# Layer 2's exponentials added by VectorE alone, and a regrouping of copies and gate steps around it, in a four-layer convolution and attention kernel

## Chip, core and metric

The kernel runs on one core of one Trainium2 chip. The metric is the device time of one execution in microseconds, as the median of several executions.

## What is computed

The input x is (4, 256, 48, 48) in float32; gn is a group normalization over groups of 8 channels. Four layers are applied, each as x = x + layer(gn(x)).

```python
# layer 0: attention over 8 heads of 64, queries and keys normalized, 2304 positions
q, k, v = split(w_qkv @ x); out = w_out @ softmax(10 * l2norm(q).T @ l2norm(k)) @ v
# layer 1: gate from a max pool, a blur of stride 3 and four depthwise sums (11x3, 3x11, two skewed)
s = x_h1 + x_w1 + x_h2 + x_w2;  out = x * upsample(sigmoid(batchnorm(s)))
# layer 2: one-head attention over 2304 positions, 64 channels, batch statistics over all samples
f = theta_x @ phi_x * 64 ** -0.5;  y = softmax(f) @ g_x;  out = batchnorm(W_w @ y + W_b)
# layer 3: channel gate, 3x3 depthwise convolution, instance normalization, leaky relu
a = sigmoid(leaky(mean(x) @ w1.T) @ w2.T);  y = conv3x3(x * a) + b;  out = leaky(instancenorm(y))
```

## The kernel before

All instructions are issued by hand in an order that the program fixes; no scheduler moves them. Every engine runs its own queue in that order and waits on semaphores. PE is TensorE, DVE is VectorE, ACT is ScalarE, POOL is GpSimd and SP issues most DMAs.

**Attention (layers 0 and 2).** A unit is 384 query columns of one sample (and, in layer 0, of a pair of heads). It is worked in 9 groups of 2 key blocks of 128; one group is one slot of the loop in `attend`. In a slot, `scores` issues 16 matmul records per group into the PSUM tiles `sc`, ACT takes the exponential into `pt` (a pool of 8 buffers, 128x768 each), `add_up` adds the exponentials of the group before to `acc`, and `weigh` multiplies them with the values into `av`. Layer 0 has 16 phases (4 samples by 4 head pairs) of 6 units; layer 2 has 4 phases (samples) of 3 units.

`add_up` has two ways: groups in `u["paired"]` are first summed on POOL into a `half` tile (line 355), and DVE then adds the half to `acc` (lines 364 and 370); the others are added by DVE one exponential at a time. In layer 0 the pairs are formed for the first sample alone; in layer 2 for all groups of the first three samples and four groups of nine of the last.

**Side work.** `fills` and `due` are tables from slot to jobs. Jobs in `fills` carry a rank: those below 1 run before `add_up`, the others after it, in order of rank. All side products on PE share two PSUM tiles (`pj_tile`), so a product can start only when the tile used two products earlier has been read. In layer 2 the side work is: the next sample's projections (`project2`: `both` for theta and phi, `g` for the values), the statistics of W times y (`w_stats`: 8 matmuls at line 1256 and two `bn_stats` at line 1264), and the whole of layer 1 for the last sample, as generators: `maxima`, the depthwise sums on PE (`strips_pe`, line 1061, from buffers named y, t and w in `ORDER3`), `gated` and its statistics. `follow` then projects the last sample for layer 2. In the last slot of a phase the generators are run to their end. A unit ends with `take` (av to `raw` on ACT), `fold` and `divide` (lines 417 to 423, on POOL, on DVE in the last sample) and a total over `acc` (`total`, or `total_here` at line 429 in the last sample).

**Layer 3.** Tiles are 8 (4 samples by 2 channel halves) of 6 convolution steps each, `products` at line 1884. A step reads shifted copies `sh` of the padded input `pad`: 12 copies for the upper and 12 for the lower half of the rows, 8 of them as DMAs from SP and 4 on engines, placed by `spread_first`, `spread_out` and `keep_here` with the table `HERE`. `grow` (line 1713, DVE) makes the padded input from PE's product at line 1651. Events are sorted by step and by a rank (CONV early, PLACE and LAST late). A chain of small steps per sample (`Chain`, times in `GATE_AT`) makes the channel gate; `scale` (ACT, line 1973), `leak` and `gain` (DVE, lines 1979 and 1984) and `store` finish a tile.

Of the kernel before, what the change touches and what calls it, by code (L numbers as in the profile page):

```python
# [78 lines left out]
def usual_path(  # L79
# [269 lines left out]
    def add_up(u, g):  # L349
# [10 lines left out]
        if g == NG - 1:  # L360
            ready, u["terms"] = ready + u["terms"], []
        if "acc" not in u and len(ready) > 1:
            u["acc"] = apool.tile([P, 2, SL], F32, tag="acc", name="acc")
            nc.vector.tensor_add(u["acc"], ready[0], ready[1])  # L364
            ready = ready[2:]
# [59 lines left out]
    def total_here(u):  # L425

        ps = pj_tile()
        for h, c in enumerate(HALVES):
            nc.tensor.matmul(ps[c, :SL], lhsT=ones, rhs=u["acc"][:, h, :], start=True, stop=True)
        u["rinv"] = rpool.tile([P, SL], F32, tag="rinv", name="rinv")  # L430
        if u.get("final"):
            fold(u, nc.vector)
            row = xsp.tile([P, NK, SL + 1], F32, tag="xs", name="lrow")[:, 0, :SL]
            nc.scalar.copy(row, ps[:, :SL])
        nc.vector.reciprocal(u["rinv"], ps[:, :SL])
        u["l"] = row if u.get("final") else ps

# [24 lines left out]
    def last(u, t):  # L462

        take(u)
        if u.get("soon"):
            todo = [
                (fills, 1, lambda: total_here(u)), (due, 2, lambda: divide(u, nc.vector)),
            ]
            if u.get("final"):
                noted.append(lambda: note(u))  # L470
            else:
                todo.insert(1, (due, 2, lambda: fold(u, nc.vector)))
                todo.append((due, 2, lambda: note(u)))
# [13 lines left out]
    def attend(phases):  # L487
# [59 lines left out]
        pu, pg = prev  # L547
        add_up(pu, pg)
        for j in range(pg * G, (pg + 1) * G):
            weigh(pu, j)  # L550
# [389 lines left out]
    def strips(b, k, norm, res):  # L940
# [52 lines left out]
        (0, 1, "y"), (0, 2, "y"), (0, 3, "y"), (0, 0, "t"), (1, 1, "w"), (1, 0, "t"), (1, 2, "w"),  # L993
        (1, 3, "t"),
    ]
# [126 lines left out]

    def gated(b, k, norm, res):

# [4 lines left out]
        )  # L1129
        yield 1  # L1130
        nc.scalar.activation(gate, acc, AF.Exp, bias=nb1[:, k : k + 1], scale=-1.0)
# [11 lines left out]
        for i in range(4):  # L1143
            if i < 3:
                nc.vector.tensor_mul(xg[:, :, i], xg[:, :, i], up)
            if i > 0:
                nc.vector.tensor_add(xg[:, :, i - 1], xg[:, :, i - 1], up2)
            yield 1


    def project2(b, norm, s2):
# [43 lines left out]
        def both(s):  # L1195
# [16 lines left out]
            )  # L1212
            nc.sync.dma_start(s2["k"][theta, cols], s2["k"][phi, cols])

        def g(s):
# [13 lines left out]
            )  # L1229
            if b == 0 and s + 2 < NSL:  # L1230
                fetch(s + 2)

        return start, [
            [(1, lambda s=s: both(s)), (2 if b else 2.7, lambda s=s: g(s))] for s in range(NSL)
        ]

# [56 lines left out]
    def l2_unit(b, c, s2):  # L1293
        return {
            "pt": {}, "qc": slice(c * SL, (c + 1) * SL), "of": s2, "after": [],
            "paired": PAIRED if b == B - 1 else range(NG), "scale": D ** -0.5,
            "soon": b == B - 1, "final": b == B - 1 and c == L2C - 1,
            "o": lambda: y_of(b)[:, c * SL : (c + 1) * SL],
        }
# [71 lines left out]
    def l1_last(b, ahead):  # L1371
# [29 lines left out]
        def gates():  # L1401
            for k in range(NK):
                yield from until(res[k], "summed")
                yield from gated(b, k, norm, res[k])
                yield from stats(k)
# [21 lines left out]
    def follow(start, slices, norm):  # L1427

        while "nb" not in norm:
            yield 1  # L1430
        yield 2
        start()
# [73 lines left out]
    for b in range(B):  # L1506
        work, others = {}, []

        def stats(b, c):
            return [lambda k=k: w_stats(b, k, c) for k in range(NK)]  # L1510

# [41 lines left out]
    for s in range(NCH):  # L1553
        projs[0]["values"](s)
    projs[1]["norms"]()
    attend(phases)
# [188 lines left out]

    def place(i, h, j, q, how):
        to = shifted[(2 * i + h) % 3][32 * q : 32 * q + 32, j, :CL]
        c0 = h * HB * W2 + SHIFT[j, q]
        fr = pads[i % NPAD][32 * j : 32 * j + 32, c0 : c0 + CL]
        if how == "sp":  # L1750
# [20 lines left out]
    def spread_first(h):  # L1771
# [4 lines left out]
        else:  # L1776
            how = dict.fromkeys(AWAY, "sp")
            how |= {(0, 0): "dve", (1, 1): "pool", (2, 2): "dve", (3, 3): "pool"}
        for (j, q), e in how.items():
            place(0, h, j, q, e)  # L1780

# [241 lines left out]
    def judge():  # L2023
# [20 lines left out]

        return [(0, MID, lows), (2, SMALL, count), (3, MOMENTS, read), (5, MID, compare)]

    GATE_AT = {
        0: (3, 5, 6, 9, 10, 11, 11, 12), B - 1: (-2, -1, 0, 3, 4, 5, 7, 8),
    }
# [19 lines left out]
    for c in range(L2C):  # L2069
        grow(1, c, ahead[c])  # L2070
        square(1, c)
    noted[0]()
    border(1)
# [13 lines left out]
    def put_before(t, i):  # L2087
# [13 lines left out]
        (-6, 0, (0, 1), "dve"), (-5, 0, (2, 3), "dve"),  # L2101
        (-3, 1, (0, 1), "act"), (-2, 1, (2,), "act"), (-2, 1, (3,), "dve"),
    ]

    def put_tile(i, t, cv, final):
# [33 lines left out]
    for i, cv in enumerate(convs):  # L2139
# [4 lines left out]
        if i:  # L2144
            for h in range(2):
                at(max(0, t - 6 + 3 * h), PLACE, lambda i=i, h=h: spread_out(i, h))
            for dt, h, js, how in HERE:
                at(t + dt, PLACE, lambda i=i, h=h, js=js, how=how: keep_here(i, h, js, how))
# [886 lines left out]
```

## Time and profile before

| | us |
|---|---|
| median of 3 executions (lowest, highest) | 3455.24 (3453.64, 3456.24) |
| the profiled execution: its time | 3453.34 |
| its span, first to last instruction | 3451.5 |
| mean granted TensorE clock | 0.997 |

The profile is of one execution. A group row gives the line, engine and operation, output and input, their shapes and the count; then total busy time in us and the mean of one in ns; then the engine's idle time just before, with what ended it. A waits row gives the total in us, the number of waits and the longest. A window row gives the stretch and its length, then the busy time of PE, PE's weight loads, DVE, ACT and POOL with counts, the granted clock, the DMA share and GB/s.

### The profile page before, as it was taken

Reading aid. Unit: us, or ns where it says so; the run is one execution under the profiler, and the core shown is the slowest. Engines: PE = TensorE matmul, PEld = TensorE weight load, DVE = VectorE, ACT = ScalarE, POOL = GpSimd, SP = SyncE. Lnnn points to the kernel's source line nnn. Section 1 sums busy time; section 2 is a strip of 40 time slices with the busy share of each in tenths; the row PEclk is TensorE's granted clock in tenths of the full one; section 3 lists DMA queues with packets and bytes.
Section 4 is the critical chain, followed back from the end, with each engine's and each line's share of the span. In section 5 each row is a group of like instructions: output and inputs, shape, how many; then the busy total and the mean of one; then the engine's idle time right before and its main releaser. Section 6 shows DMA issues by size and latency. Waiting matters only on the chain. (4 is left out here: it accounts for less than half of the span.)

```text
span 3451.5 us, 89291 instructions
## 1 busy us (share of the span) xinstructions
PE 3384.6 (98%) x37966; PEld 1698.6 (49%) x37966; DVE 2539.3 (74%) x3298; ACT 2297.4 (67%) x3690; POOL 828.0 (24%) x734
## 2 busy tenths in 40 slices
PE   8999999999999999999999999999999999899988
PEld 5555555555545444544454445554444444444533
DVE  3455545568788788687888787878887878857777
ACT  5565655555886687557866885569768855454577
POOL 2433333320111111011110010101010114777434
PEclk9999999999999999999999999999999999999999
DMA  2211111111111111131111011111111110230067
GB/s 91 50 23 27 22 27 22 27 22 27 20 32 22 27 22 22 31 73 22 27 21 24 15 31 18 31 18 27 22 27 18 29 21 8 58 66 11 9 154 229
DMA packets 111593, 127.25 MB, mean 37 GB/s; under 512 B 42912, under 2 KB 101648, under 8 KB 110416
## 3 DMA queue, kind: packets, MB, share of 16 engines
q1 hardware_dynamic: 109936, 119.53, 17.3%
q8 instruction: 300, 4.92, 0.6%
q10 hardware_dynamic: 1248, 1.91, 0.2%
q14 instruction: 109, 0.89, 0.1%
HBM read 56.99 MB, written 11.80 MB: 20 GB/s over the span
## 5 line engine op out<-in xcount | busy, mean ns | idle before, releaser
L330 ACT ACTIVATE pt<-sc 128x768 f32<-128x768 f32 x1944 | 1473.6, 810 | 757.9 <-PE sc L324 751.4
L370 DVE TENSOR_TENSOR acc<-acc,pt 128x768 f32<-128x768 f32 x1368 | 1367.3, 1000 | 145.3 <-ACT pt L330 51.7
L344 PE MATMUL av<-pt,v 64*64 64x384 f32 x13824 | 1274.8, 484 | 0.0
L324 PE MATMUL sc<-q,k 64*64 64x384 f32 x13824 | 1270.0, 482 | 0.5 <-ACT pt L330 0.5
L324 PEld LDWEIGHTS sc<-q,k 64*64 64x64 f32 x13824 | 525.3, 133 | 589.6 <-issue 556.5
L344 PEld LDWEIGHTS av<-pt,v 64*64 64x64 f32 x13824 | 518.2, 133 | 568.4 <-issue 521.5
L421 POOL TENSOR_TENSOR o<-o,rinv 128x384 f32<-128x384 f32 x95 | 123.7, 1302 | 1710.1 <-DMA rinv<-rinv 1700.0
L355 POOL TENSOR_TENSOR half<-pt 128x768 f32<-128x768 f32 x189 | 370.7, 1966 | 488.0 <-ACT pt L330 405.3
L739 DVE SCALAR_TENSOR_TENSOR x<-pj,bo,x 128x384 f32<-128x384 f32 x192 | 118.5, 617 | 344.2 <-ACT row L388 186.9
L951 ACT ACTIVATE prod<-pd,wt 128x256 f32<-128x256 f32 x486 | 340.5, 761 | 0.2
L370 DVE TENSOR_TENSOR acc<-acc,half 128x768 f32<-128x768 f32 x171 | 187.5, 1097 | 167.8 <-POOL half L355 166.7
L625 PE MATMUL pj<-xs,w 128*128 128x384 f32 (+1 forms) x720 | 275.4, 505 | 0.0
L625 PEld LDWEIGHTS pj<-xs,w 128*128 128x128 f32 x720 | 124.1, 189 | 127.9 <-ACT v L664 34.3
L324 PE MATMUL sc<-qv,kd 64*64 64x384 f32 x1728 | 167.3, 492 | 2.9 <-ACT pt L330 2.8
L974 DVE TENSOR_REDUCE prod<-prod 128x256 f32<-128x1280 f32 x114 | 168.7, 1480 | 0.9 <-ACT prod L951 0.9
L344 PE MATMUL av<-pt,qv 64*64 64x384 f32 x1728 | 167.1, 490 | 0.0
L723 PE MATMUL pj<-o,wo 128*128 128x384 f32 (+1 forms) x384 | 161.4, 502 | 2.3 <-DVE x L739 2.0
L659 PEld LDWEIGHTS pj<-w,xs 128*128 128x128 f32 x1080 | 134.4, 191 | 24.2 <-issue 1.2
L364 DVE TENSOR_TENSOR acc<-pt 128x768 f32<-128x768 f32 x99 | 116.4, 1176 | 39.5 <-ACT pt L330 39.4
L659 PE MATMUL pj<-w,xs 128*128 128x128 f32 x1080 | 134.9, 275 | 0.0
L417 POOL TENSOR_TENSOR o<-raw 128x384 f32<-128x384 f32 x95 | 121.6, 1280 | 43.6 <-ACT raw L413 42.5
L413 ACT COPY raw<-av 128x768 f32<-128x768 f32 x108 | 86.4, 800 | 48.2 <-PE av L344 47.7
(304 smaller groups left out, 2227.6 us busy)
## 6 DMA issues: line engine op xcount, KB each, us to landing
xs<-in_x_dram SPq DMA_DIRECT2D x90, 384.0 KB
sh<-pad SPq DMA_DIRECT2D x126, 162.2 KB
rinv<-rinv SPq DMA_DIRECT2D x208, 94.5 KB
out_dram<-x SPq DMA_DIRECT2D x23, 384.0 KB
w<-in_wqkv_dram SPq DMA_DIRECT2D x32, 192.0 KB
x<-in_x_dram SPq DMA_DIRECT2D x4, 1152.0 KB
x<-in_x_dram SPq DMA_DIRECT2D x9, 384.0 KB
rinv<-ls SPq DMA_DIRECT2D x208, 1.5 KB
```

The costliest lines, as they stand in the source:

```text
L324: nc.tensor.matmul(ps[c * D : (c + 1) * D, h, :SL], lhsT=u["of"]["k"][r, j0 : j0 + D], rhs=u["of"]["q"][r, u["qc"]], start=True, stop=True,)
L330: nc.scalar.activation(pt, ps[:, :, :SL], AF.Exp, scale=u["scale"])
L344: nc.tensor.matmul(u["av"][h * D : (h + 1) * D, half, :SL], lhsT=value(u, j, h)[r], rhs=pt[r, h, :], start=j == 0, stop=j == JB - 1,)
L355: nc.gpsimd.tensor_add(half, pts[0], pts[1])
L370: nc.vector.tensor_add(u["acc"], u["acc"], term)
L417: eng.tensor_add(u["sum"], u["raw"][:, 0, :], u["raw"][:, 1, :])
L421: eng.tensor_mul(o, o, u["rinv"])
L625: nc.tensor.matmul(ps[:, :n], lhsT=at["w"][:, k, t, :], rhs=xs[s][:, k, :n], start=k == 0, stop=k == NK - 1,)
L659: nc.tensor.matmul(ps[:, i * P : (i + 1) * P], lhsT=xs[s][:, k, i * P : (i + 1) * P], rhs=at["w"][:, k, 2, :], start=k == 0, stop=k == NK - 1,
L723: nc.tensor.matmul(ps[:, :n], lhsT=wo[:, p, k * P : (k + 1) * P], rhs=o["o"][:, :n], start=True, stop=True,)
L951: nc.scalar.activation(bufs[n % 3][:, :, min(n, 1) + i].rearrange("p (r c) -> p r c", c=AS), pd[:, PAD + dr : PAD + dr + AS, PAD + dc : PA ...
L974: nc.vector.tensor_reduce(to, bufs[n % 3][:, :, : min(n, 1) + len(taps)], AX.X, ALU.add)
```

## The change

In layer 2 no group is paired any more: DVE adds every exponential. The last unit's last group is not added by DVE at all: `total_here` sums it on PE and is issued before the last `weigh`, and the row copy for the final check is issued on ACT after `take`. `w_stats` gets rank 0.5. In the projections of the first sample `g` goes before `both`. `gated` yields less often in the last sample, `follow` starts a slot earlier, and one stack of the depthwise sums uses the y buffer. In layer 3 the first tile's upper copies are made in two parts (500 and 798 columns), two of its lower copies are made by DVE later, each tile's lower copy j = 1 goes from ACT to DVE a step later, the last tile's lower copies are all on DVE, the last gate chain's sum over groups comes a step later, and a comparison of the final check moves to a later rank. `of_k.clear()` gives one small product its own PSUM tile.

```diff
@@ -361,2 +361,5 @@
             ready, u["terms"] = ready + u["terms"], []
+            if u.get("final"):
+                u["loose"] = ready
+                return
         if "acc" not in u and len(ready) > 1:
@@ -427,11 +430,12 @@
         ps = pj_tile()
-        for h, c in enumerate(HALVES):
-            nc.tensor.matmul(ps[c, :SL], lhsT=ones, rhs=u["acc"][:, h, :], start=True, stop=True)
+        terms = [u["acc"], *u.get("loose", ())]
+        for i, term in enumerate(terms):
+            for h, c in enumerate(HALVES):
+                nc.tensor.matmul(
+                    ps[c, :SL], lhsT=ones, rhs=term[:, h, :], start=i == 0,
+                    stop=i == len(terms) - 1,
+                )
         u["rinv"] = rpool.tile([P, SL], F32, tag="rinv", name="rinv")
-        if u.get("final"):
-            fold(u, nc.vector)
-            row = xsp.tile([P, NK, SL + 1], F32, tag="xs", name="lrow")[:, 0, :SL]
-            nc.scalar.copy(row, ps[:, :SL])
         nc.vector.reciprocal(u["rinv"], ps[:, :SL])
-        u["l"] = row if u.get("final") else ps
+        u["l"] = ps
 
@@ -464,5 +468,9 @@
         take(u)
+        if u.get("final"):
+            row = xsp.tile([P, NK, SL + 1], F32, tag="xs", name="lrow")[:, 0, :SL]
+            nc.scalar.copy(row, u["l"][:, :SL])
+            u["l"] = row
         if u.get("soon"):
             todo = [
-                (fills, 1, lambda: total_here(u)), (due, 2, lambda: divide(u, nc.vector)),
+                (due, 2, lambda: fold(u, nc.vector)), (due, 2, lambda: divide(u, nc.vector)),
             ]
@@ -471,3 +479,3 @@
             else:
-                todo.insert(1, (due, 2, lambda: fold(u, nc.vector)))
+                todo.insert(0, (fills, 1, lambda: total_here(u)))
                 todo.append((due, 2, lambda: note(u)))
@@ -548,2 +556,3 @@
         add_up(pu, pg)
+        total_here(pu)
         for j in range(pg * G, (pg + 1) * G):
@@ -993,3 +1002,3 @@
         (0, 1, "y"), (0, 2, "y"), (0, 3, "y"), (0, 0, "t"), (1, 1, "w"), (1, 0, "t"), (1, 2, "w"),
-        (1, 3, "t"),
+        (1, 3, "y"),
     ]
@@ -1122,3 +1131,3 @@
 
-    def gated(b, k, norm, res):
+    def gated(b, k, norm, res, brief=False):
 
@@ -1129,3 +1138,4 @@
         )
-        yield 1
+        if not brief:
+            yield 1
         nc.scalar.activation(gate, acc, AF.Exp, bias=nb1[:, k : k + 1], scale=-1.0)
@@ -1147,3 +1157,4 @@
                 nc.vector.tensor_add(xg[:, :, i - 1], xg[:, :, i - 1], up2)
-            yield 1
+            if not brief or i % 2:
+                yield 1
 
@@ -1213,2 +1224,4 @@
             nc.sync.dma_start(s2["k"][theta, cols], s2["k"][phi, cols])
+            if b == 0 and s + 2 < NSL:
+                fetch(s + 2)
 
@@ -1229,7 +1242,6 @@
             )
-            if b == 0 and s + 2 < NSL:
-                fetch(s + 2)
 
         return start, [
-            [(1, lambda s=s: both(s)), (2 if b else 2.7, lambda s=s: g(s))] for s in range(NSL)
+            [(1, lambda s=s: both(s)), (2, lambda s=s: g(s))] if b else
+            [(1, lambda s=s: g(s)), (2.7, lambda s=s: both(s))] for s in range(NSL)
         ]
@@ -1295,3 +1307,3 @@
             "pt": {}, "qc": slice(c * SL, (c + 1) * SL), "of": s2, "after": [],
-            "paired": PAIRED if b == B - 1 else range(NG), "scale": D ** -0.5,
+            "paired": (), "scale": D ** -0.5,
             "soon": b == B - 1, "final": b == B - 1 and c == L2C - 1,
@@ -1403,3 +1415,3 @@
                 yield from until(res[k], "summed")
-                yield from gated(b, k, norm, res[k])
+                yield from gated(b, k, norm, res[k], brief=True)
                 yield from stats(k)
@@ -1430,3 +1442,3 @@
             yield 1
-        yield 2
+        yield 1
         start()
@@ -1509,3 +1521,3 @@
         def stats(b, c):
-            return [lambda k=k: w_stats(b, k, c) for k in range(NK)]
+            return [(0.5, lambda k=k: w_stats(b, k, c)) for k in range(NK)]
 
@@ -1554,2 +1566,3 @@
         projs[0]["values"](s)
+    of_k.clear()
     projs[1]["norms"]()
@@ -1745,6 +1758,6 @@
 
-    def place(i, h, j, q, how):
-        to = shifted[(2 * i + h) % 3][32 * q : 32 * q + 32, j, :CL]
+    def place(i, h, j, q, how, part=slice(0, CL)):
+        to = shifted[(2 * i + h) % 3][32 * q : 32 * q + 32, j, part]
         c0 = h * HB * W2 + SHIFT[j, q]
-        fr = pads[i % NPAD][32 * j : 32 * j + 32, c0 : c0 + CL]
+        fr = pads[i % NPAD][32 * j : 32 * j + 32, c0 + part.start : c0 + part.stop]
         if how == "sp":
@@ -1777,5 +1790,7 @@
             how = dict.fromkeys(AWAY, "sp")
-            how |= {(0, 0): "dve", (1, 1): "pool", (2, 2): "dve", (3, 3): "pool"}
-        for (j, q), e in how.items():
-            place(0, h, j, q, e)
+            how |= {(1, 1): "pool", (3, 3): "pool"}
+        top = (RS + 2) * W2
+        for part in (slice(0, CL),) if h else (slice(0, top), slice(top, CL)):
+            for (j, q), e in how.items():
+                place(0, h, j, q, e, part)
 
@@ -2044,6 +2059,6 @@
 
-        return [(0, MID, lows), (2, SMALL, count), (3, MOMENTS, read), (5, MID, compare)]
+        return [(0, MID, lows), (2, SMALL, count), (3, MOMENTS, read), (9, LAST, compare)]
 
     GATE_AT = {
-        0: (3, 5, 6, 9, 10, 11, 11, 12), B - 1: (-2, -1, 0, 3, 4, 5, 7, 8),
+        0: (3, 5, 6, 9, 10, 11, 11, 12), B - 1: (-2, 0, 1, 4, 4, 5, 7, 8),
     }
@@ -2071,2 +2086,3 @@
         square(1, c)
+    keep_here(0, 1, (0, 2), "dve")
     noted[0]()
@@ -2101,4 +2117,5 @@
         (-6, 0, (0, 1), "dve"), (-5, 0, (2, 3), "dve"),
-        (-3, 1, (0, 1), "act"), (-2, 1, (2,), "act"), (-2, 1, (3,), "dve"),
+        (-3, 1, (0,), "act"), (-2, 1, (2,), "act"), (-2, 1, (3,), "dve"), (-1, 1, (1,), "dve"),
     ]
+    HERE_LAST = [*HERE[:2], (-3, 1, (0, 1), "dve"), (-2, 1, (2, 3), "dve")]
 
@@ -2146,3 +2163,3 @@
                 at(max(0, t - 6 + 3 * h), PLACE, lambda i=i, h=h: spread_out(i, h))
-            for dt, h, js, how in HERE:
+            for dt, h, js, how in HERE_LAST if i == len(convs) - 1 else HERE:
                 at(t + dt, PLACE, lambda i=i, h=h, js=js, how=how: keep_here(i, h, js, how))
```

## The prediction

> **What bounds the kernel now.** First the page's busy times: TensorE (PE) is busy for 98% of the span, so a change gains only where PE idles or runs at a reduced clock.
>
> ```profile
> PE 3384.6 (98%) x37966; PEld 1698.6 (49%) x37966; DVE 2539.3 (74%) x3298; ACT 2297.4 (67%) x3690; POOL 828.0 (24%) x734
> ```
>
> Then the windows view says where. I cut at the first scores of layer 2's four samples (2870.6, 2977.9, 3092.5, 3202.0), the last scores (3282.0), the first full convolution (3305.5) and the last (3429.1). The first columns are length and PE busy; then PEld, DVE, ACT, POOL, clock, DMA.
>
> ```profile
> 0.00:2704.00 2704.00, 2693.83 (x29826) 1357.57 (x29830) 1975.15 (x2572) 1852.82 (x3009) 473.67 (x411) 1.00 0.15 29
> 2704.00:2870.57 166.57, 161.70 (x1959) 77.83 (x1955) 135.06 (x173) 109.16 (x164) 15.08 (x11) 1.00 0.14 22
> 2870.57:2977.90 107.33, 98.62 (x1164) 48.90 (x1160) 99.59 (x110) 53.84 (x81) 73.06 (x38) 0.98 0.14 25
> 2977.90:3092.50 114.60, 107.67 (x1384) 54.62 (x1380) 69.88 (x77) 56.59 (x89) 80.45 (x45) 1.00 0.31 65
> 3092.50:3202.00 109.50, 100.39 (x1196) 53.58 (x1192) 72.53 (x90) 54.34 (x83) 74.73 (x40) 0.95 0.13 21
> 3202.00:3282.00 80.00, 77.88 (x946) 42.74 (x942) 63.59 (x74) 42.23 (x57) 42.35 (x40) 1.00 0.04 5
> 3282.00:3305.50 23.50, 16.34 (x147) 9.46 (x140) 20.12 (x46) 14.83 (x14) 7.54 (x8) 1.00 0.20 49
> 3305.50:3429.10 123.60, 118.11 (x1337) 47.49 (x1337) 89.39 (x127) 106.21 (x188) 59.61 (x143) 1.00 0.88 235
> ```
>
> Length less PE busy: layer 2 idles 8.7, 6.9, 9.1 and 2.1 = 26.8 us, against 10.2 in the first 2704. PE's waits in layer 2:
>
> ```profile
> PE pj L1256 <- DVE bst L1264: 7.2, 4, 3.5
> PE pj L1061 <- DVE bst L1264: 4.0, 2, 2.3
> PE sc L324 <- ACT pt L330: 2.8, 1, 2.8
> PE pj L233 <- DVE bst L1264: 2.5, 1, 2.5
> ```
>
> Behind nearly all stands VectorE (DVE): a projection's PSUM tile is freed by bn_stats late in DVE's queue. Why DVE is late although 74% busy, the groups show: the add that takes 0.96-0.99 us elsewhere (second line: layer 0, POOL nearly idle) takes 1.28 beside POOL's pair sums, and DVE also sat 46 us waiting for them.
>
> ```profile
> L370 DVE TENSOR_TENSOR acc<-acc,half 128x768 f32<-128x768 f32 x74 | 94.8, 1282 | 47.4 <-POOL half L355 46.4
> ...
> L370 DVE TENSOR_TENSOR acc<-acc,pt 128x768 f32<-128x768 f32 x380 | 375.6, 988 | 42.1 <-ACT pt L330 17.5 <-DVE acc L370 0.5
> ...
> L355 POOL TENSOR_TENSOR half<-pt 128x768 f32<-128x768 f32 x93 | 194.6, 2101 | 106.8 <-ACT pt L330 85.4 <-DVE acc L370 9.0 <-DMA stack<-pd 5.3
> ```
>
> The longest wait in the timeline, a 0.95 us add stretched to 2.55 with bn_stats and PE behind it:
>
> ```profile
> 3133.89 4.87 POOL L355 TENSOR_TENSOR half<-pt 128x768 f32<-128x768 f32 x2 [0.96 <-DVE acc L364]
> ...
> 3137.03 2.55 DVE L370 TENSOR_TENSOR acc<-acc,half 128x768 f32<-128x768 f32 x1
> 3139.50 1.02 DVE L1264 BATCH_NORM_STATS2 bst<-pj 128x6 f32<-128x384 f32 x2
> 3139.72 1.80 POOL L355 TENSOR_TENSOR half<-pt 128x768 f32<-128x768 f32 x1 [0.96 <-DVE acc L370]
> 3140.11 2.01 PE L1256 MATMUL pj<-y,Ww 64*64 64x384 f32 x8 [3.51 <-DVE bst L1264]
> ```
>
> **The Trainium skill.** "SBUF — State Buffer", section "Who interferes with whom": a DVE instruction with two SBUF inputs and a GpSimd instruction that reads SBUF exclude each other for a whole instruction. The trace agrees: 2.55 against 0.95. "TensorE: Matmul & The Clock Gate", section "What's actually happening": an idle window of about 3.4 us halves PE's clock. The trace halves it already after waits of 2.8, 3.5 and 2.5 us: the clock is 0.73, 0.66 and 0.79 over the 6.4, 10 and 8 us around them, a further loss near 1.7, 3.4 and 1.7 us.
>
> **The change, part by part** (minus is faster).
>
> *Exponentials on DVE alone.* POOL loses 93 pair sums (194.6 us). DVE's adds per unit go from 8 (three units in each of samples 0-2) and 13 (last sample) to 17, the final unit 15: 111 to 202, +91. Free of POOL each costs 0.96 us. The other DVE work of the four windows, taken row by row at its duration where POOL rests (L893 1.38 us, here 2.66; L917 0.58, here 2.09; L260 0.16, here 1.78), sums to 44, 27, 30 and 22 us. POOL work that stays (73.1 - 59.4 = 13.7 us in the first window, about 24, 18 and 18 after; half sums at 2.05) still blocks: in the first window DVE exceeds its free sum by 99.6 - (23 x 0.96 + 44) = 33 us over 73 us of POOL, 0.45 each. DVE after:
> - first: 51 x 0.96 + 44 + 6 = 99 us, PE 98.6: a tie. DVE, not PE, may set the pace. Of the 8.7 idle and 1.7 clock I take -4 (bounds -8 to +6).
> - second: 49 + 27 + 11 = 87 of PE 107.7. Waits of 1.5, 2.3 and 1.9 go: -5.
> - third: 49 + 30 + 8 = 87 of PE 95 at full clock. The waits of 3.5 and 2.5 and 5.1 us of clock: -11. But the brief gates bunch: their eleven DVE operations of 0.35 to 1.75 us now come in about half the slots, so sums queue behind them and I return 2. Projections no longer all stand in the last slot (PE waits 5 x 0.42 and 1.0): -1. Together -10.
> - fourth: 47 + 22 + 8 = 77 of PE 77.9, another tie: -1 of the two waits near 1.05.
>
> The statistics' products at rank 0.5 put bn_stats ahead of the slot's two sums (1.9 us), which is what PE waits for; the sums behind it are needed only when exponential buffers (eight, two per group) come round, about two slots of 2.58 us later. That is the cover; if DVE stands over 5 us behind, it is gone. Sum of layer 2: **-20** (-27 to +2).
>
> *Layer 0's last pair.* g goes before theta/phi. PE waits 6 x 0.62 = 3.7 us at L1221 for two 0.58 us evictions; one 0.32 us copy then frees the tile, 0.83 earlier. Late next is L739's 0.62 us (PE waited 0.9 for it once). **-2.5** (-4 to +1). SP's order of the copies is the same.
>
> *Last unit.* The last group's two exponentials go to PE directly, four more matmuls. Now: exponential ends 3282.9, three sums to 3286.1, L429, a row copy, reciprocal to 3290.1, y products 3291.2. Then: L429 at about 3283.2, 0.87 + 8 x 0.16 = 2.2 us, reciprocal to 3288.0; meanwhile the av products (1.3), raw (0.8), fold 0.55, two y operations 1.0, products at 3289.6: **-1.6** (0 to -2.5; lost if DVE is 1.6 late).
>
> *Layer 3.* The first copies in two parts: SP issues 12 instead of 6 DMAs at 0.63 us. The top six arrive hardly earlier, since issue sets the pace (sixth issued 3.2 us after the first either way, shorter transfer -0.3); the bottom six and everything queued behind on SP come about 3 us later (12 x 0.63 against 6 x 0.73 with today's transfers): the second row block about when it is needed, the other half's eight (needed 3.6 us after their arrival now) just in time. +0.5 (-1 to +4). One copy per tile: ACT loses 1.27 us, DVE gains 0.83, with ACT 106 of 123.6 busy and DVE 89. PE's waits at L1651 (1.9 and 1.1) are DVE waiting for ACT's scale, which stood behind the sh copies: -2 (-3 to +1). On POOL the last gate chain a slot later removes PE's 2.0 us wait at L1803; shift and scale of tile 5 then go ahead of it on POOL. The end hangs on DVE, which also gets three copies (2.5 us), covered by its 6.75 us wait for ACT near 3406 and its 2.5 us wait for hraw: -1.5. **-3** (-7 to +4). One stack copy to "y" and of_k.clear(): 0, within +-0.5; PE's neighbours cover them.
>
> Sum: -20 - 2.5 - 1.6 - 3 = -27. The profiled execution took 3453.34 us (span 3451.5 and 1.8 around it), 1.9 below the median of 3455.24. On the median: **3428 us**.
>
> **Rivals.**
> - *DVE becomes the bound of layer 2* in the tied windows, and bn_stats still arrive late in bunches: the second and third windows give half (-8), the first and fourth nothing, the rest -4: 3443. For it: 99 against 98.6 and 77 against 77.9. Against: layer 0 from the second sample on runs such sums at up to 2.48 us of DVE in 2.58 us slots without PE waits.
> - *Slower: the sums stay blocked.* If an add keeps 1.28 us and the other rows their blocked times (72.7 us in the first window), DVE there needs 51 x 1.28 + 73 = 138 us of 107.3: +31, less about 10 won elsewhere: 3476. It decides from about 127 us of DVE in that window, where +20 eats the rest of the gain. Against: POOL's reading falls from 73 to 14 us there.
> - *No effect:* waits move from bn_stats to other PSUM tiles of the same lane (slots keep their length), layer 3 cancels: 3453. Against: the 26.8 us idle have one cause.
>
> **How the numbers follow.** Forecast 0.63, DVE-bound 0.22, slower 0.09, no effect 0.06. A measurement of this kernel can tell about 0.2% (7 us) from no change: faster 0.85, same 0.06, slower 0.09. Range: layer 2's -27 with -8 elsewhere gives 3420, a little more 3417; the DVE-bound case up to -8 gives 3447.
>
> **What would show it.** Right: in the groups L370 near 0.96-1.05 us and no half rows; PE idle in the third window below 4 us at clock 0.99 or more; L1256 waits under 3 us in sum; no L1803 wait at the end. Wrong: PE's waits on ACT pt (buffers held by DVE) above 8 us; DVE over 110 us in the first window; PE waiting for sh DMAs by more than 3 us at the start of layer 3.

## The result, and the profile after

| | before | after |
|---|---|---|
| device time, median | 3454.44 us (3452.76 to 3456.24) | 3423.78 us (3422.10 to 3426.00) |
| ratio, 95% interval | | 0.9912 (0.9894 to 0.9929) |
| profiled execution: span, time | 3451.5, 3453.34 us | 3422.8, 3424.57 us |

The kernel became 30.7 us faster; 3428 was forecast, with a range of 3417 to 3447. The kernel before has four executions here: the three of the table above and one of 3452.76. Of the profile after, the page's first line of busy times:

```profile
PE 3381.9 (99%) x37974; PEld 1680.7 (49%) x37974; DVE 2549.1 (74%) x3399; ACT 2284.3 (67%) x3684; POOL 632.2 (18%) x643
```

TensorE (PE) is busy nearly as long as before (3384.6), in a span that is 28.7 us shorter. POOL lost 196 us and DVE, which took over its additions (and some copies in layer 3), gained only 10. The windows view of the kernel after, cut at the same events: the start of layer 0's last phase, the first scores of layer 2's four samples, the last scores, the first full convolution, the last (columns: length, then PE, PEld, DVE, ACT, POOL, clock, DMA share and GB/s):

```profile
0.00:2693.55 2693.55, 2686.77 (x29747) 1355.56 (x29751) 1970.82 (x2567) 1846.46 (x3000) 467.35 (x409) 1.00 0.15 29
2693.55:2862.45 168.90, 166.89 (x2034) 81.30 (x2030) 140.99 (x178) 114.32 (x173) 16.07 (x13) 1.00 0.16 27
2862.45:2965.13 102.68, 98.15 (x1163) 47.66 (x1159) 89.67 (x137) 53.81 (x81) 18.04 (x13) 0.98 0.13 24
2965.13:3074.77 109.64, 107.72 (x1384) 53.58 (x1380) 82.59 (x112) 56.56 (x89) 21.76 (x17) 1.00 0.34 71
3074.77:3177.18 102.41, 97.18 (x1196) 46.14 (x1192) 72.10 (x111) 54.52 (x83) 15.12 (x12) 1.00 0.13 21
3177.18:3253.52 76.34, 76.32 (x944) 35.48 (x940) 62.63 (x83) 42.14 (x57) 19.10 (x28) 1.00 0.04 5
3253.52:3275.20 21.68, 17.83 (x157) 9.35 (x148) 17.44 (x45) 13.57 (x14) 5.70 (x8) 1.00 0.08 18
3275.20:3404.80 129.60, 122.94 (x1337) 46.15 (x1337) 101.53 (x152) 96.22 (x183) 68.50 (x145) 0.97 0.85 233
```

Cut at those events in both traces, the span's loss of 28.7 us divides so:

| stretch | before | after | change | forecast |
|---|---|---|---|---|
| up to layer 0's last phase | 2697.8 | 2693.6 | -4.2 | 0 |
| layer 0's last phase | 172.8 | 168.9 | -3.9 | -2.5 |
| layer 2, sample 0 | 107.3 | 102.7 | -4.6 | -4 |
| sample 1 | 114.6 | 109.6 | -5.0 | -5 |
| sample 2 | 109.5 | 102.4 | -7.1 | -10 |
| sample 3 | 79.9 | 76.3 | -3.6 | -1 |
| last scores to last convolution | 147.2 | 151.3 | +4.1 | -4.6 with the row below |
| last convolution to the end | 22.4 | 18.0 | -4.4 | (of the -4.6, the last unit -1.6) |

In layer 2 the groups (by form; the last column is idle time before them, and for whom) show that all additions are now from exponentials straight into the sum, at the unhindered duration:

```profile
L373 DVE TENSOR_TENSOR acc<-acc,pt 128x768 f32<-128x768 f32 x190 | 187.8, 988 | 35.6 <-ACT pt L330 24.5
...
L367 DVE TENSOR_TENSOR acc<-pt 128x768 f32<-128x768 f32 x12 | 12.8, 1064 | 12.9 <-ACT pt L330 12.9
```

202 additions, as counted ahead, where the half rows took 1282 ns. PE's waits in layer 2 (us in total, times, longest):

```profile
PE pj L247 <- DVE lsum L447: 3.1, 1, 3.1
PE pj L1234 <- ACT qv L1220: 2.2, 6, 0.4
PE sc L324 <- ACT pt L330: 1.8, 5, 0.4
PE pj L233 <- DVE bst L1276: 1.5, 1, 1.5
```

The 13.7 us that PE stood for the bn_stats behind the output products, the diagonal products and L233 are down to 1.5. Two waits came in their place. The one at L247, for DVE at the start of sample 0, is 3.1 us where that product waited 1.2 us for the same line before, and PE's clock was half for 3.4 us with it, a loss of 1.7. The other is in layer 3, where PE's waits and the timeline show one that the kernel before did not have:

```profile
PE cv L1899 <- ACT hraw L1842: 4.0, 1, 4.0
```

```profile
3383.07 0.39 PE L1835 MATMUL cv<-pm,w 128*64 128x1 f32 x4 [0.49 <-POOL pm L1830]
...
3387.29 0.14 ACT L1842 COPY hraw<-cv 64x1 f32<-64x1 f32 x1
...
3387.47 5.35 PE L1899 MATMUL cv<-sh,taps 96*32 96x384 f32 x32 [4.01 <-ACT hraw L1842]
```

The small product L1835 of the last gate chain lies in the free columns of a convolution's PSUM bank. With the chain moved, ScalarE's read of it (hraw) was issued in the same slot, ahead of the convolution of the odd step that writes that bank. So the convolution had to wait for a 0.14 us copy that stood in ScalarE's queue. PE's clock was then half for 6.8 us, a further loss of 3.4.

### The profile page after: what moved, and what is told of

Its sections match the earlier page's. It is cut to its first block, busy times and chain, and to the rows that moved or that the text cites. A ratio compares the mean times of both kernels' runs of the same rounds, so it can differ in the third digit from the quotient of the medians.

```text
span 3422.8 us, 89318 instructions
## 1 busy us (share of the span) xinstructions
PE 3381.9 (99%) x37974; PEld 1680.7 (49%) x37974; DVE 2549.1 (74%) x3399; ACT 2284.3 (67%) x3684; POOL 632.2 (18%) x643
## 4 chain that ended last, share of the span: by engine, by line
PE 92%; DVE 3%; POOL 1%; ACT 1%; issue 1%; SPq 0%; DMA 0%; DVEq 0%; POOLq 0%; ACTq 0%
PE av L344 36%; PE sc L324 35%; PE pj L634 8%; PE pj L732 4%; PE pj L668 4%; DVE acc L373 2%; PE pj L386 1%; PE cv L1899 1%; PE pj L1210 1%; PE pj L1070 1%; PE pj L1268 0%; PE pj L1234 0%; SPq L1057 0%; SPq L1764 0%; DMA sh<-pad 0%
## 5 line engine op out<-in xcount | busy, mean ns | idle before, releaser
L373 DVE TENSOR_TENSOR acc<-acc,pt 128x768 f32<-128x768 f32 x1534 | 1524.6, 994 | 178.4 <-ACT pt L330 76.2
L355 POOL TENSOR_TENSOR half<-pt 128x768 f32<-128x768 f32 x96 | 176.0, 1833 | 378.2 <-ACT pt L330 323.5
L373 DVE TENSOR_TENSOR acc<-acc,half 128x768 f32<-128x768 f32 x96 | 91.7, 956 | 120.5 <-POOL half L355 120.2
L324 PE MATMUL sc<-qv,kd 64*64 64x384 f32 x1728 | 159.4, 483 | 1.8 <-ACT pt L330 1.8
L367 DVE TENSOR_TENSOR acc<-pt 128x768 f32<-128x768 f32 x108 | 127.8, 1183 | 35.0 <-ACT pt L330 34.8
```

The source lines that it names most:

```text
L324: nc.tensor.matmul(ps[c * D : (c + 1) * D, h, :SL], lhsT=u["of"]["k"][r, j0 : j0 + D], rhs=u["of"]["q"][r, u["qc"]], start=True, stop=True,)
L355: nc.gpsimd.tensor_add(half, pts[0], pts[1])
L373: nc.vector.tensor_add(u["acc"], u["acc"], term)
```

## The experiments

Theory: the pair sums on GpSimd and the additions on DVE held each other up by reading at the same time; the rest of the gain comes from three single waits of PE (the value products at the start, layer 0's last phase, layer 3), each with a cause of its own. Rivals: the chain of dependencies through GpSimd's half sums cost the time, or the shorter gate steps and the earlier statistics did the work. The medians in the table stand each beside runs of the kernel before on the same chip (3453.96 for the first four rows, 3454.21 for the next four, 3454.62 for three, 3455.40 for the last). Two kernels' medians less than 2 us apart are not told apart here. The writes have two executions, the others four or more.

| run | median, us | ratio to before (95%) | layer 2, us |
|---|---|---|---|
| pair sums back | 3445.00 | 0.9973 (0.9963 to 0.9984) | 409.4 |
| pair edit alone, on before | 3434.30 | 0.9941 (0.9924 to 0.9957) | 395.2 |
| after, with reads by GpSimd | 3507.38 | 1.0153 (1.0136 to 1.0170) | 475.3 |
| after, with writes by GpSimd | 3425.88 | 0.9919 (0.9899 to 0.9939) | 392.2 |
| no of_k.clear() | 3428.57 | 0.9929 (0.9912 to 0.9945) | 390.6 |
| old order of the products | 3430.31 | 0.9931 (0.9914 to 0.9947) | 392.4 |
| hraw a slot later | 3425.95 | 0.9923 (0.9906 to 0.9939) | 390.5 |
| gate chain at its old times | 3423.21 | 0.9910 (0.9893 to 0.9926) | 391.3 |
| layer 3's copies on ScalarE | 3428.33 | 0.9923 (0.9910 to 0.9937) | 391.5 |
| first copies in one part | 3423.63 | 0.9910 (0.9897 to 0.9924) | 393.5 |
| statistics on DVE | 3422.61 | 0.9905 (0.9890 to 0.9921) | 391.9 |
| waits moved | 3421.40 | 0.9903 (0.9886 to 0.9919) | 390.2 |

Layer 2 took 411.4 us before and 391.1 after.

### Pair sums back, and the pair edit alone

```diff
# on the kernel after                     (the second run: the reverse edit, on the kernel before)
-            "paired": (), "scale": D ** -0.5,
+            "paired": PAIRED if b == B - 1 else range(NG), "scale": D ** -0.5,
```

> The kernel after, with the pair sums of layer 2 given back to GpSimd in the old pattern (every group in samples 0 to 2, four of nine in sample 3) and everything else of the change kept. Theory (the pair sums were the cause: DVE reads and POOL reads hold each other up, and DVE has to wait for each half sum): layer 2 gets back most of its 20 us, so about 3424 + 17 = 3441 us, with adds of half rows of about 1280 ns and a sum of PE idle in the four samples of about 25 us in place of 11.7. Rival (the shorter gate steps and the statistics ahead of the adds, which stay in, did the work in layer 2): 3424 to 3429 us.

> The kernel before with one edit, layer 2's adds by DVE alone. Theory: layer 2 loses 14 to 20 us by itself, so 3435 to 3440 us, and the rest of the stretches are as before. Rival (DVE needs the other edits too: without the statistics ahead of the adds and the short gate steps it becomes late, and PE waits at the statistics' banks): 3445 to 3455 us, with waits of PE for DVE at L1265 (the output product) and L233 over 8 us in sum.

Undone in the kernel after, the edit costs 21.2 us; alone in the kernel before it brings 19.7. Layer 2 has 18.3 and 16.2 us of these. The other edits move layer 2 by 2.0 us without it (411.4 to 409.4) and 4.1 with it (395.2 to 391.1). PE idles 24.5 us in layer 2 with the pair sums back (25 expected, 11.7 after). With the edit alone its waits at the output product and L233 are 0.9 and 3.3 us, so DVE is in time there without the other edits. The rival of the gate steps and statistics is refuted as the main cause: the pair edit is the cause of most of the gain in layer 2, and the other edits have 2 to 4 us of it. The groups with the pair sums back are much as before (the add and its idle time, then POOL's pair sum):

```profile
L373 DVE TENSOR_TENSOR acc<-acc,half 128x768 f32<-128x768 f32 x74 | 100.9, 1364 | 42.7 <-POOL half L355 41.5
...
L355 POOL TENSOR_TENSOR half<-pt 128x768 f32<-128x768 f32 x93 | 196.7, 2123 | 103.2 <-ACT pt L330 79.8 <-DVE acc L373 8.0 <-issue 6.1
```

That leaves two readings of the same rows: the add is long (1364 ns), or it is the chain through the half sums that costs, for which DVE waits 41.5 us.

### GpSimd reads beside DVE, GpSimd writes beside DVE

Both keep DVE's additions as they are after the change and give GpSimd 93 instructions that nothing depends on.

```diff
         pts = [u["pt"][j] for j in range(g * G, (g + 1) * G)]
+        if g in u.get("ghost", ()):      # the groups that were paired before
+            spare = hpool.tile([P, 2, SL], F32, tag="half", name="spare")
+            nc.gpsimd.tensor_add(spare, pts[0], pts[1])     # the second run: nc.gpsimd.memset(spare, 0.0)
```

> The kernel after, and beside it GpSimd adds the same pairs as before into half tiles that nothing reads (93 sums). DVE does all its adds and depends on none of them. Theory A (what held layer 2 up was the two engines reading at once): DVE's adds beside a pair sum take 1.28 us and more in place of 0.99, that is 93 times 0.3 or some 28 us more of DVE in layer 2, PE waits again for banks that DVE frees, and the time is 3432 to 3450 us. Theory B (it was the chain from ScalarE's tile over GpSimd's half sum to DVE's add, which is gone here too): adds stay at 0.99 us and the time is 3422 to 3427 us.

> The kernel after, and beside it GpSimd fills 93 half tiles with zeros, as many and as large as the outputs of the old pair sums, at the same places in its order, without reading anything. Theory A (it is the reading beside each other that costs): adds stay at about 0.99 us and the time at 3422 to 3427 us. Rival (any access of GpSimd to the memory, or its being busy ahead of its other work, costs): adds at 1.1 us or more and 3430 us or more.

With the reads the kernel is 83.6 us slower than after, and 53 slower than before. Groups in layer 2 (up to 7 us before its end), the kernel with the reads:

```profile
L376 DVE TENSOR_TENSOR acc<-acc,pt 128x768 f32<-128x768 f32 x186 | 253.0, 1360 | 19.0 <-ACT pt L330 7.6
...
L354 POOL TENSOR_TENSOR spare<-pt 128x768 f32<-128x768 f32 x92 | 195.3, 2130 | 121.8 <-ACT pt L330 117.0 <-ACT row L394 4.6
```

and the kernel with the writes:

```profile
L376 DVE TENSOR_TENSOR acc<-acc,pt 128x768 f32<-128x768 f32 x190 | 193.5, 1018 | 35.1 <-ACT pt L330 23.9
...
L354 POOL MEMSET spare<- 128x768 f32 x93 | 65.5, 739 | 0.4
```

An add takes 1360 ns beside reading pair sums and 1018 beside writes of the same tiles, where the whole kernel takes 3425.88 us, as theory A had it. The writes keep GpSimd busy for 65.5 us only, a third of the 195.3 us of the pair sums; an estimate from these numbers is that, if writing held the adds up as reading does, they would take some 1113 ns (988 and a third of the 372 that the reads add). They don't. DVE depends on no half sum in either run, so reading at the same time is enough to hold layer 2 up, without the chain through the half sums. This is what the Trainium skill, "SBUF — State Buffer", section "Who interferes with whom", states: a DVE instruction with two SBUF inputs contends with GpSimd's reads, not with its writes. The theory's size was far too small (8 to 26 us expected): DVE fills 121.4 us of the first sample's window, which grows to 131.0, and PE then waits in new places. Its waits in layer 2 of the kernel with the reads begin:

```profile
PE sc L324 <- ACT pt L330: 21.5, 11, 7.8
PE pj L1271 <- DVE bias L1188: 9.3, 1, 9.3
```

The first line is ScalarE without a free exponential buffer. ScalarE itself waited 27.5 us for buffers that DVE's late additions held, and 9.0 us for buffers that GpSimd had still to read; so a part of the 83.6 us may come of GpSimd as a late reader, and not of the longer additions. How much the dependence on the half sums cost by itself in the kernel before stays open; no run took the contention away and left the dependence.

### The start: no of_k.clear()

```diff
-    of_k.clear()
     projs[1]["norms"]()
```

> The kernel after without the line of_k.clear(). Theory: the value products of the first pair (72 matmuls in the trace of after) again have one PSUM buffer in place of two, PE waits 5 times about 0.57 us for ScalarE's eviction between them, some 3 to 4 us with what follows, and nothing after 50 us changes: 3427 to 3428.5 us. Rival (the 4 us ahead of the last phase of layer 0 come from the adds and gates later on): the same as after, 3422 to 3426 us, and the start of the last phase of layer 0 at 2693.5 us.

It costs 3.8 us by the last phase's start (2697.3 against 2693.6) and 4.8 in the median. The first 45 us of its timeline have the value products of the first pair in bits of 12 matmuls (two of the six bits shown):

```profile
31.15 1.50 PE L668 MATMUL pj<-w,x 128*128 128x128 f32 x12
33.22 1.60 PE L668 MATMUL pj<-w,x 128*128 128x128 f32 x12 [0.57 <-ACT v L673]
```

against one run in the kernel after:

```profile
31.55 8.20 PE L668 MATMUL pj<-w,x 128*128 128x128 f32 x72
```

The dictionary held the PSUM tile of the last k product, because projs[1]["norms"]() puts a small product into its free columns. So one of the two pj buffers was taken, and each product of a slice waited for the eviction of the one before. The kernel before showed the same five waits at L659.

### Layer 0's last phase: the old order

```diff
-            [(1, lambda s=s: both(s)), (2, lambda s=s: g(s))] if b else
-            [(1, lambda s=s: g(s)), (2.7, lambda s=s: both(s))] for s in range(NSL)
+            [(1, lambda s=s: both(s)), (2 if b else 2.7, lambda s=s: g(s))] for s in range(NSL)
```

with fetch moved back into g.

> The kernel after with the old order in the last pair of layer 0's following phase (the two q and k products of a slice ahead of its value product, with the fetch in the value step). Theory: the last phase of layer 0 gets back 3.9 us (PE waits at five of the slices about 0.6 us each for ScalarE), and the rest is as in after: 3426 to 3428 us. Rival (those 3.9 us come from the shorter gate steps, which stay): 3422 to 3425 us and a last phase of 168.9 us.

The last phase takes 172.8 us again, and PE's first wait in it is that of before, which the kernel after hasn't got:

```profile
PE pj L1231 <- ACT qv L1220: 3.7, 6, 0.6
```

The whole is 6.5 us slower, more than the 3.9. Of the rest, 1.5 us are in sample 2, where the clock was half for 3.4 us after the same wait of 1.53 us (L233) that cost no clock in the profile of after.

### Layer 3: the gate chain's times

```diff
-        0: (3, 5, 6, 9, 10, 11, 11, 12), B - 1: (-2, 0, 1, 4, 4, 5, 7, 8),
+        0: (3, 5, 6, 9, 10, 11, 11, 12), B - 1: (-2, 0, 1, 4, 5, 6, 7, 8),      # hraw and hl a slot later; the second run: (-2, -1, 0, 3, 4, 5, 7, 8)
```

> The kernel after with the last gate chain's times (-2, 0, 1, 4, 5, 6, 7, 8) in place of (-2, 0, 1, 4, 4, 5, 7, 8): ScalarE's read of the small product (hraw) is put a slot later, behind the convolution that writes the same PSUM bank, and the step after it too. Theory: the wait of 4.0 us of a convolution (L1899) for hraw goes, and with it the 6.8 us at half clock that follow it (3.4 us lost): 3416 to 3420 us. Rival (PE was waiting for an engine that is late anyway, the evictions of ScalarE, so that the wait moves to the next eviction or to the second small product): 3422 to 3425 us with a wait of 3 us or more at another line.

> The kernel after with the last gate chain at its old times (-2, -1, 0, 3, 4, 5, 7, 8). Theory: the wait for hraw of 4.0 us goes (the old read lies behind the convolution of the odd slot), the wait for gn_sq on GpSimd of about 2 to 3 us comes back with a stretch at half clock: 3420 to 3425 us, so the move of the chain by itself brought nothing or cost up to 3 us. Rival, as the prediction had it (the later chain is worth 1.5 us): 3425 to 3427 us.

Putting hraw behind the convolution did not help (3425.95). The bank was free, but PE now waited for hl, the next step of the chain (on DVE), which waits for hraw. PE's waits in layer 3, and ScalarE's timeline, of that run:

```profile
PE cv L1852 <- DVE hl L1847: 3.9, 1, 3.9
```

```profile
3392.89 1.03 ACT L1988 ACTIVATE x<-x,in_sf,in_sc 128x768 f32<-128x768 f32 x1 [5.80 <-POOL in_sf L1982]
3393.82 0.14 ACT L1842 COPY hraw<-cv 64x1 f32<-64x1 f32 x1
```

hraw stands in ScalarE's queue behind a scaling (L1988) that waits 5.8 us for in_sf, the shift of a finished tile and the end of GpSimd's small statistics. So the bank was only where the lateness showed; ScalarE's queue, and in it the wait for GpSimd, is behind it. The timeline of GpSimd in the kernel after has the same instruction twice, first while DVE was idle and then while it worked on two-input instructions:

```profile
3379.35 0.19 POOL L1938 TENSOR_TENSOR in_mv<-in_mv,in_d 128x1 f32<-128x1 f32 x1
...
3387.60 0.97 POOL L1938 TENSOR_TENSOR in_mv<-in_mv,in_d 128x1 f32<-128x1 f32 x1
```

At the old times the kernel is as fast as after (3423.21). PE's wait for gn_sq (the chain's sum of squares, from GpSimd) is back with 2.9 us, that for hraw is gone, and moving the chain brought nothing that the medians show.

### Layer 3: the copies, and the first copies

```diff
# copies: three edits back to those of before for every tile but the first
-        (-3, 1, (0,), "act"), (-2, 1, (2,), "act"), (-2, 1, (3,), "dve"), (-1, 1, (1,), "dve"),
+        (-3, 1, (0, 1), "act"), (-2, 1, (2,), "act"), (-2, 1, (3,), "dve"),
-    HERE_LAST = [*HERE[:2], (-3, 1, (0, 1), "dve"), (-2, 1, (2, 3), "dve")]
+    HERE_LAST = HERE
```

> The kernel after with layer 3's shifted copies of every tile but the first where they were: two or three by ScalarE, the last tile's like the others. Theory formed from the traces of the last runs: GpSimd's small steps of the tile statistics take 0.19 us alone and 0.7 to 1.6 us beside DVE's copies and two-input work, so with fewer copies on DVE the chain to in_sf is ready sooner: ScalarE's waits for in_sf on GpSimd fall from 16.4 us in layer 3 to about 8 (7.7 in the kernel before), PE's wait of 4.0 us for hraw falls to under 2, and the time is 3419 to 3423 us. The prediction's view (ScalarE is relieved by 2 us by the copy that moved): 3425 to 3427 us.

```diff
# first copies in one part
-            how |= {(1, 1): "pool", (3, 3): "pool"}
-        top = (RS + 2) * W2
-        for part in (slice(0, CL),) if h else (slice(0, top), slice(top, CL)):
+            how |= {(0, 0): "dve", (1, 1): "pool", (2, 2): "dve", (3, 3): "pool"}
...
-    keep_here(0, 1, (0, 2), "dve")
```

> The kernel after with layer 3's first copies in one part each as before, four by DVE and GpSimd at once in place of two DVE copies put later. The prediction took the two parts for 0.5 us slower: 3423 to 3424 us. Rival, from the trace of after, where the first convolutions start 20.8 us after the last scores in place of 23.6 us: the two parts are worth 1 to 3 us at the start of layer 3, and the time is 3425 to 3427 us, with the first convolution 22 us or more after the last scores.

The copies' run refutes half of the theory it was to test. With fewer copies on DVE, GpSimd's part went as expected; ScalarE's waits in layer 3 of the kernel after, then of this run:

```profile
ACT x L1988 <- POOL in_sf L1982: 16.4, 6, 5.8
```

```profile
ACT x L1988 <- POOL in_sf L1982: 6.3, 3, 2.3
```

But hraw was later still, since ScalarE now had its own copies ahead of it; its timeline in this run:

```profile
3388.89 2.55 ACT L1766 COPY sh<-pad 32x1298 f32<-32x1298 f32 x2
...
3392.40 0.14 ACT L1842 COPY hraw<-cv 64x1 f32<-64x1 f32 x1
```

PE waited 6.7 us for hraw, and the kernel was 4.6 us slower than after. With the gate chain moved, the copies thus belong on DVE.

From the last scores to the end, before took 169.6 us; with the moved copies and the old gate times 168.0; with both moved 169.2; with the gate chain moved and the old copies 172.7. These are single profiles and scatter: runs with the layer 3 of after unchanged took from 168.4 (the writes) to 172.8 us (pair sums back), and the pair edit alone, whose layer 3 is that of before, took 168.0. So of the four only what the medians repeat is shown: the 4.6 us of the copies with the chain moved. The old copies with the old gate times, beside the other edits of layer 3, were not run; what the copies bring without the moved chain is not shown.

The first copies in two parts let the first products of the convolution start 20.8 us after the last scores, against 21.8 in one part; the median is the same (3423.63). What begins earlier is given back within the layer.

### Two versions

The first moves the small statistics of the last three tiles but the final one to DVE, with hraw and hl a slot later; the second has these, hl a slot earlier again (-2, 0, 1, 4, 5, 5, 7, 8), and moves two more waits.

```diff
-        at(t + 8, FRONT, lambda: cv.moments(nc.gpsimd))
-        at(t + 8, MOMENTS, cv.scales)
-        at(t + 8, LAST, cv.shift)
+        eng = nc.vector if i >= len(convs) - 3 else nc.gpsimd
+        at(t + 8, FRONT, lambda: cv.moments(eng))
+        at(t + 8, MOMENTS, lambda: cv.scales(eng))
+        at(t + 8, LAST, lambda: cv.shift(eng))
```

> The kernel after with the gate times (-2, 0, 1, 4, 5, 6, 7, 8) and the small steps of the statistics of the last three tiles but the final one (moments, scales, shift) by DVE in place of GpSimd. Theory (hraw and hl are late because ScalarE's queue stands for in_sf, and in_sf is late because GpSimd's steps are slowed beside DVE): about 12 steps of 0.16 us on DVE, ScalarE's waits for in_sf under 8 us in sum in place of 16.4, PE's waits of 4.0 us for hraw or hl under 1 us, and no half clock ahead of 3400 us: 3415 to 3420 us. Rival (DVE is the late engine of layer 3, and waits now itself for the reciprocal roots that GpSimd still makes): 3423 to 3428 us, with new PE waits for DVE's copies (sh L1770).

```diff
# on top of that
         u["l"] = ps
+        if "final" not in u:
+            u["l"] = hpool.tile([P, 2, SL], F32, tag="half", name="lsums")[:, 0, :]
+            nc.scalar.copy(u["l"], ps[:, :SL])
...
-                (due, 2, lambda: fold(u, nc.vector)), (due, 2, lambda: divide(u, nc.vector)),
+                (due, 2 if "final" in u else 1, lambda: fold(u, nc.vector)),
+                (due, 2, lambda: divide(u, nc.vector)),
...
-                todo.append((due, 2, lambda: note(u)))
+                todo.append((due, 2 if "final" in u else 3, lambda: note(u)))
...
-                [(SMALL, first_layer)], [(MOMENTS, hidden)], [(MID, leaky)],
+                [(SMALL, first_layer)], [(MOMENTS, hidden)],
+                [(PLACE if self.n == B - 1 else MID, leaky)],
```

> The kernel of the statistics on DVE (gate times -2, 0, 1, 4, 5, 5, 7, 8) with two more edits. hl is made a slot earlier, behind DVE's leaks of that slot and ahead of its copies. At the end of layer 0, the sums of the last unit are copied by ScalarE into memory, so that their PSUM bank comes free without DVE, DVE folds the unit's halves one slot earlier and notes its sums one slot later: its eviction L748 comes some 1.7 us sooner. Theory (what is left of the waits is the order of in-order queues, and a wait of 1.6 us and more costs again as much at half clock): PE's wait of 1.65 us for hl goes with its 3.4 us at half clock, and the wait of 3.1 us at L247 falls to under 1.8 us with 3.4 us at half clock or none after it in place of 6.8: 3415 to 3419 us. Rival (each wait only makes room for the next: the next eviction, the next copy): 3420 to 3424 us.

Statistics on DVE: 3422.61 us, inside neither expectation. PE's wait for hl fell from 3.9 us (hraw a slot later) to 1.7, and ScalarE's for in_sf on GpSimd only to 10.0, as the earlier tiles' statistics are still GpSimd's.

Waits moved: 3421.40 us (3420.72 to 3421.74), all its executions below the lowest of after, though the two ratios' intervals overlap. The time lies with the rival; of the theory's details, sample 0 went from 102.7 to 100.6 us, and in place of the 3.1 us at L247 PE waits, as the timeline has it,

```profile
2872.90 0.91 PE L736 MATMUL pj<-o,wo 128*128 128x384 f32 x2 [1.89 <-DVE x L752]
```

for the same DVE queue. From the last scores to the end it takes 166.9 us, against 169.2 in after. It is the fastest kernel of the study by median. Of the 5 to 9 us below after that its expectation asked for, 2.4 came, and it is 1.2 us from the statistics on DVE, too little to be told apart; waits such as this one took the place of those removed.

## Why the prediction was right, and where it was not

**Layer 2, -20: -20.3.** That the pair sums were the cause is shown by putting them back, and that their reading beside DVE is enough by the reads and the writes; how the gain divides between shorter additions and the half sums that DVE no longer waits for is not. Within the sum, sizes were off. DVE's windows were put at 99, 87, 87 and 77 us and measured 89.7, 82.6, 72.1 and 62.6. The adds were right (51.3 us in the first window, 49 forecast); the term that was mis-sized is the rest, forecast with its surcharge for POOL at 50, 38, 38 and 30 us, and 38.4, 29.6, 21.0 and 17.5 by the trace. So the ties of the first and fourth windows were none: the fourth gave 3.6 us in place of 1, and PE idles 0.02 us in it. The third gave 7.1 in place of 10. Two errors of 2.6 and 2.9 us thus cancel, and that the sum fits to 0.3 is luck. In the third PE idles 5.2 us, not under 4 as was to show it right (1.5 at L233, 1.1 for DVE's sum at L386, 1.3 at L1210), and got back 3.2 us of its busy time where the term for the clock had 5.1. The output products' waits for bn_stats are gone, as was to be seen. That "the 26.8 us idle have one cause" was too strong: bn_stats ended 13.7 us of it, and 11.7 us are left, 3.5 of them for ScalarE's evictions (L1234, L1210). How much of the 2 to 4 us of the other edits in layer 2 is the rank of the statistics and how much the brief gates was not tried.

**Layer 0's last pair, -2.5: -3.9.** Six waits of 0.62 went whole; the eviction that was expected to be late next showed up once, with 1.6 us. It lay within the bounds given.

**of_k.clear(), 0 within 0.5: about -4.** This step failed. "PE's neighbours cover them" was given no reason of its own; the long first window idles so little in proportion (10.2 of 2704 us) that nothing stands out in it. In the first 45 us of the timeline before, five waits of 0.57 us at L659, each with ScalarE's eviction as its releaser, have no neighbour that covers them.

**Last unit, -1.6: -0.3.** The output products begin 8.9 us after the last scores in place of 9.3. The condition that was named came true: DVE was late, and L434 waited 1.0 us for the sum of the group before.

**Layer 3, -3: about 0.** From 169.6 to 169.2 us with the last unit in it, less than single profiles of the same layer 3 differ by. The step that failed is the gate chain (-1.5 forecast; 3423.78 us with its move, 3423.21 without): the wait for gn_sq did fall from 2.0 to 0.9 us, but what the move put in its place was not followed. hraw's place in ScalarE's queue, and which bank it reads, decide; that is 4.0 us of waiting and a slower clock. The copies' -2 is not shown: they are worth 4.6 us where the chain is moved, in part since on ScalarE they stand ahead of hraw, and what they are worth without it was not run. Their reading was half right: ahead of PE's wait of 1.9 us at L1651 DVE had waited 1.6 us for ScalarE's scale, but ahead of that of 1.1 us it had waited for a DMA of shifted copies:

```profile
3389.04 1.14 DVE L1713 SCALAR_TENSOR_TENSOR pad<-w,sc,x 128x384 f32<-128x384 f32 x2 [1.87 <-DMA sh<-pad]
```

After, PE waits 0.6 us in sum there. Moving copies to DVE also had a price that was not in the sum: GpSimd's small steps are slowed beside DVE, and ScalarE waits for them 16.4 us in place of 7.7.

**The rivals.** The DVE-bound case asked for 99 us of DVE against 98.6 of PE; it was 89.7. The slower case, additions that stay blocked, did not occur, but the run with GpSimd's reads is its mechanism: 3507 us where 3476 was worked out, since all four windows grow and not only the first. The errors of the two missed terms, 4 us for of_k.clear() and 3 for layer 3, had opposite signs, so the sum was nearer than its parts; that too is luck.

## What to carry to other kernels

Before splitting additions between DVE and GpSimd, price the reading side: two engines with two inputs each can be slower together than one alone, and an instruction that nobody waits for is enough. When a step of an in-order queue is moved, follow where its first reader then stands in the reader's queue, and which bank it reads. Look at short stretches by themselves: five waits of 0.6 us in the first 45 us of a 3454 us execution cost, with what hung on them, about 4 us, a seventh of this change's gain.

## What the hardware showed that was not expected

GpSimd's instructions on one column per partition (128x1) took 0.19 us with DVE idle and 0.7 to 1.0 us beside DVE's large instructions; a chain of some fifteen of them stretches by several microseconds. PE's clock went to half for 3.4 us after waits as short as 1.53 us (L233, with the old order of the products) and 1.65 us (hl, with the statistics on DVE), and after the same 1.53 us at L233 it stayed full in the profile of after. The Trainium skill, "TensorE: Matmul & The Clock Gate", section "What's actually happening", describes a free-running window of 3.4 us as the measure; the half-clock stretch after each of these waits, 3.4 us, and the variation from kernel to kernel fit a window with no fixed place, but the waits that halved the clock are shorter than the idle window it names.
